# Attention with a checked bound in place of row maxima, three heads at a time on TensorE tiles, and denominators summed on VectorE

## The chip, the core and the metric

The kernel runs on one core of a Trainium2 chip. Times are device microseconds (us) of whole executions. Executions of one kernel spread, so differences of medians of up to some 20 us are read with care. Shorter is better. Engines are named as in the profile: PE is TensorE (matmuls), PEld its weight loads, DVE VectorE, ACT ScalarE, POOL GpSimd, SP SyncE.

## The reference

Two layers over 8 sequences of 1024 tokens with 128 channels, all in fp32. Only the first part of layer 0, attention with four heads of 32 channels, is touched by the change:

```python
def l2norm(t, axis=1, eps=1e-12):                 # axis 1: over the tokens, not the channels
    return t / jnp.clip(jnp.linalg.norm(t, ord=2, axis=axis, keepdims=True), eps)
qkv = jnp.einsum('bxyc,cf->bxyf', x, w_qkv)       # x has been group-normed
q, k, v = ...                                     # (B, 1024, 4 heads, 32)
attn = jnp.einsum('bihd,bjhd->bhij', l2norm(q), l2norm(k)) * 10.0
attn = attn - attn.argmax(axis=-1, keepdims=True) # a shift per row: softmax takes no notice
attn = jax.nn.softmax(attn, axis=-1)
out = jnp.einsum('bhij,bjhd->bhid', attn, v)      # then w_out, b_out and the residual
# [cut: layer 1, a state-space mixer in two directions and a spectral filter]
```

## The kernel before

Attention computes the scores twice: once with queries in rows, only for their row maxima (`peaks`), and once transposed, keys in rows, for the exponentials (`attend`). The negated maxima are written as a 33rd row behind a head's 32 query channels, against a row of ones in the keys, so that the transposed scores come out less their maximum. Behind each head's 32 value channels stand 32 columns of ones, so that the values matmul yields the denominators too.

```python
# peaks: one key-major pass per head for the maxima
sc = ps_s.tile([P, T], F32, tag="s", ...)
for n in range(2):
    nc.tensor.matmul(sc[:, n * 512 : (n + 1) * 512], lhsT=q[rows, h // 2, i * P : (i + 1) * P],
                     rhs=k[rows, h // 2, n * 512 : (n + 1) * 512], start=True, stop=True)
nc.vector.tensor_reduce(top[:, i : i + 1], sc, AX.X, ALU.max, negate=True)
# [cut: the maxima are turned into a row by a diagonal and a one-row matmul]

# attend: two key tiles of one head, half of its queries
rows = slice((h % 2) * 64, (h % 2) * 64 + DH + 1)          # 33 rows
for i in range(2):
    j = 2 * n + i
    nc.tensor.matmul(pt[:, i, :], lhsT=k[rows, h // 2, j * P : (j + 1) * P],
                     rhs=q[rows, h // 2, cols], start=True, stop=True)
nc.scalar.activation(pr, pt, AF.Exp)                        # [shapes cut]
yield
for i in range(2):
    j = 2 * n + i
    nc.tensor.matmul(po, lhsT=v[:, j, h, :], rhs=pr[:, i, :],   # 64 columns: values, ones
                     start=(j == 0), stop=(j == NT - 1))
# [cut: copy, reciprocal of the denominators, product, output projection, residual]
```

Before attention begins, `select_bank` mixes four candidate filter banks for layer 1 on GpSimd, in operations of 128x2048 elements:

```python
def mixed(src, dst, n, tag):
    for i in range(NM):
        part = pool.tile([P, n, C], F32, tag=tag, name=tag)     # one buffer
        nc.sync.dma_start(part, src[i].rearrange("k d e -> d k e"))
        to = dst if i == 0 else part
        nc.gpsimd.tensor_scalar(to, part, w[:, i : i + 1], None, ALU.mult)
        if i:
            nc.gpsimd.tensor_tensor(dst, dst, part, ALU.add)
```

## Time and profile before

| | before |
|---|---|
| time, median of 3 runs | 5078.32 us (5063.51 to 5088.73) |
| span of the profiled execution | 5048.0 us |
| attention, from the start to the fetch of layer 1's filter taps | 2449 us |
| the rest | 2599 us |
| granted PE clock within attention (300 to 550 us) | 0.67 |

The lines of the page that carry this stand in the prediction below.

### The profile page before, as it was taken

The page shows a single profiled execution, that of the slowest core. Times are in us where ns is not written, and L with a number is a line of the kernel's source. Part 1 is how long each engine was busy: PE and PEld are TensorE (multiplying, and loading weights), DVE is VectorE, ACT ScalarE, POOL GpSimd, SP SyncE. Part 2 cuts the span into 40 slices and gives each one's busy share as a digit, 9 for nine tenths or more (in the row PEclk, how much of TensorE's full clock was granted, in tenths as well). Part 3 has the DMA queues.
Part 4 walks back from the last instruction along what each step waited for, and adds up shares of the span by engine and source line. Part 5 has one row for each costly group of instructions (what it writes and reads, how often), then busy time and mean ns, then how long its engine had stood idle before and what let it go on. Part 6 is the DMA issues. An engine that isn't in the chain of part 4 may idle for free.

```text
span 5048.0 us, 32979 instructions
## 1 busy us (share of the span) xinstructions
PE 4862.9 (96%) x12896; PEld 2143.7 (42%) x12896; DVE 1659.0 (33%) x2454; ACT 1102.5 (22%) x1648; POOL 925.7 (18%) x1125
## 2 busy tenths in 40 slices
PE   4999999999999999999889998989999999999999
PEld 1222222222222222222355555555555555555555
DVE  2232322223232222322577777773111111111111
ACT  0111111111111111111456556551010010100100
POOL 7200000000000000000367777671000000000000
PEclk6576676766667666676899999899999999999999
DMA  3000000000000000000100000001000000000000
GB/s 87 13 0 0 4 0 4 0 4 0 0 4 0 0 0 0 0 0 0 34 1 1 1 1 1 1 1 34 5 0 5 1 4 5 1 5 5 1 5 5
DMA packets 31836, 29.37 MB, mean 6 GB/s; under 512 B 4416, under 2 KB 23232, under 8 KB 31680
## 3 DMA queue, kind: packets, MB, share of 16 engines
q1 hardware_dynamic: 31680, 27.26, 1.9%
q8 instruction: 102, 1.67, 0.1%
q14 instruction: 54, 0.44, 0.0%
HBM read 23.06 MB, written 4.19 MB: 5 GB/s over the span
## 4 chain that ended last, share of the span: by engine, by line
PE 87%; POOL 6%; DVE 5%; issue 1%; DMA 1%; ACT 1%; SPq 0%; POOLq 0%; ACTq 0%; DVEq 0%
PE pu L742 22%; PE po L361 15%; PE sc L324 14%; PE pt L349 14%; PE cpo L768 9%; PE sy L647 2%; PE pk L315 2%; PE pl L618 1%; DVE bc L553 1%; DVE xs L553 1%; POOL dau L611 1%; PE sy L649 1%; PE cpo L760 1%; POOL xd L652 1%; PE pp L537 1%
## 5 line engine op out<-in xcount | busy, mean ns | idle before, releaser
L742 PE MATMUL pu<-flt,uk 128*128 128x512 f32 (+3 forms) x4096 | 1183.7, 432 | 0.0
L742 PEld LDWEIGHTS pu<-flt,uk 128*128 128x128 f32 x4096 | 770.4, 189 | 640.6 <-issue 361.8
L361 PE MATMUL po<-pr,v 128*64 128x512 f32 x1024 | 780.2, 896 | 0.0
L324 PE MATMUL sc<-k,q 32*128 32x512 f32 x1024 | 741.7, 858 | 6.4 <-DVE top L331 5.3
L349 PE MATMUL pt<-q,k 33*128 33x512 f32 x1024 | 725.1, 826 | 0.7 <-ACT q L318 0.7
L331 DVE TENSOR_REDUCE top<-sc 128x1 f32<-128x1024 f32 x256 | 310.3, 1212 | 1124.8 <-PE sc L324 1124.4
L753 DVE COPY u<-pu 128x512 f32<-128x512 f32 x256 | 177.0, 691 | 1281.0 <-PE pu L742 1281.0
L357 ACT ACTIVATE pr<-pt 128x1024 f32<-128x1024 f32 x256 | 261.9, 1023 | 1398.6 <-PE pt L349 1398.6
L751 ACT COPY u<-pu 128x512 f32<-128x512 f32 x256 | 149.8, 585 | 1434.4 <-PE pu L742 1434.4
L324 PEld LDWEIGHTS sc<-k,q 32*128 32x128 f32 x1024 | 234.4, 254 | 522.4 <-issue 475.6
L349 PEld LDWEIGHTS pt<-q,k 33*128 33x128 f32 x1024 | 204.8, 231 | 459.9 <-issue 453.0
L361 PEld LDWEIGHTS po<-pr,v 128*64 128x64 f32 x1024 | 157.7, 185 | 554.4 <-issue 537.3
L307 POOL TENSOR_TENSOR diag<-ident,top 128x512 f32<-128x512 f32 x64 | 69.9, 1093 | 1463.2 <-DVE top L331 1463.2
L369 DVE RECIPROCAL den<-av 32x512 f32<-32x512 f32 x64 | 213.8, 3341 | 334.7 <-ACT av L367 334.2
L768 PE MATMUL cpo<-u,m_even 128*128 128x512 f32 x512 | 262.1, 594 | 0.0
L768 PE MATMUL cpo<-u,m_odd 128*128 128x512 f32 x512 | 256.8, 593 | 0.0
L647 PE MATMUL sy<-xdt,lm 128*128 128x64 f32 x1024 | 145.5, 287 | 27.4 <-DVE y L654 27.3
L647 PEld LDWEIGHTS sy<-xdt,lm 128*128 128x128 f32 x1024 | 133.3, 200 | 77.2 <-issue 31.0
L553 DVE SCALAR_TENSOR_TENSOR xs<-xp,cw,xs 128x1024 f32<-128x1024 f32 x96 | 147.0, 1538 | 3.2 <-ACT xs L548 3.2
L608 POOL TENSOR_TENSOR xd<-xb,dsk 128x256 f32<-128x256 f32 x128 | 116.2, 908 | 61.3 <-DVE y L654 42.7
L318 ACT COPY q<-pk 1x512 f32<-1x512 f32 x64 | 36.9, 577 | 371.7 <-PE pk L315 371.7
L716 POOL MEMSET ut<- 128x2 f32 x8 | 0.7, 99 | 604.7 <-PE cpo L760 603.9
(200 smaller groups left out, 4174.3 us busy)
## 6 DMA issues: line engine op xcount, KB each, us to landing
flt<-in_phi_rows SPq DMA_DIRECT2D x4, 1026.0 KB, 10.7
xin<-in_x SPq DMA_DIRECT2D x8, 512.0 KB, 4.0
flt<-in_phi_rows SPq DMA_DIRECT2D x4, 1024.0 KB, 9.5
out<-res SPq DMA_DIRECT2D x8, 512.0 KB, 3.2
part_u<-in_L_ffn_M_u SPq DMA_DIRECT2D x4, 192.0 KB, 2.7
win<-in_L_attn_fwd_in_proj SPq DMA_DIRECT2D x1, 320.0 KB, 6.8
win<-in_L_attn_bwd_in_proj SPq DMA_DIRECT2D x1, 320.0 KB, 3.2
wqkv<-in_L_conv_w_qkv SPq DMA_DIRECT2D x1, 192.0 KB, 2.4
```

Source lines behind the costliest of these rows:

```text
L324: nc.tensor.matmul(sc[:, n * 512 : (n + 1) * 512], lhsT=q[rows, h // 2, i * P : (i + 1) * P], rhs=k[rows, h // 2, n * 512 : (n + 1) * 512] ...
L331: nc.vector.tensor_reduce(top[:, i : i + 1], sc, AX.X, ALU.max, negate=True)
L349: nc.tensor.matmul(pt[:, i, :], lhsT=k[rows, h // 2, j * P : (j + 1) * P], rhs=q[rows, h // 2, cols], start=True, stop=True,)
L357: nc.scalar.activation(pr.rearrange("p i t -> p (i t)"), pt.rearrange("p i t -> p (i t)"), AF.Exp)
L361: nc.tensor.matmul(po, lhsT=v[:, j, h, :], rhs=pr[:, i, :], start=(j == 0), stop=(j == NT - 1))
L369: nc.vector.reciprocal(den, av[DH : 2 * DH, :])
L553: nc.vector.scalar_tensor_tensor(acc, xp[:, at : at + T], cw[d][:, n, i : i + 1], acc, ALU.mult, ALU.add)
L647: nc.tensor.matmul(py[:, 0, hc], lhsT=lm[:, h, :], rhs=xdt[:, hc], start=True, stop=True)
L742: nc.tensor.matmul(pu[:, : HT - j * P], lhsT=uk[:, src, j, :], rhs=rows[:, k % 4, off + j * P : off + HT], start=(j == 0), stop=(j == HB - 1),
L751: nc.scalar.copy(u, pu)
L753: nc.vector.tensor_copy(u, pu)
L768: nc.tensor.matmul(po, lhsT=banks[lag][:, k, :], rhs=u, start=False, stop=last)
```

## The change

Its intent: softmax needs the row maximum only against overflow. The scores are bounded by the norms of the queries and keys, so the exponentials are taken without a shift, the bound is computed beside the rest, and a general copy of the attention and of layer 1 stands behind a branch that is taken if the bound exceeds 20. The queries and keys no longer need a spare row, so four heads fit side by side in 128 rows. Score matmuls of three different heads use three different row groups of PE, values matmuls three different column groups. The ones behind the values are gone; VectorE adds the exponentials up over the key tiles instead, and a matmul with ones sums the rest over the partitions.

```diff
-            for _ in peaks(0, 0, seqs[0]): ...          # [peaks, spare rows, ones behind values: all gone]
+            stream = [(j, h) for j in range(NT) for h in range(HEADS)]
+            groups = [stream[i : i + 3] for i in range(0, len(stream), 3)]
 # scores of one group
+                for i, (j, h) in enumerate(units):
+                    rows = slice(h * DH, (h + 1) * DH)
+                    nc.tensor.matmul(pt[:, i, :], lhsT=k[rows, j * P : (j + 1) * P],
+                                     rhs=q[rows, half * 512 : (half + 1) * 512], start=True, stop=True)
+                nc.scalar.activation(pr, pt, AF.Exp)      # [shapes cut]
 # values of one group, two groups later
+                    nc.tensor.matmul(po[rows, :], lhsT=v[:, j, rows], rhs=pr[:, i, :],
+                                     start=(j == 0), stop=(j == NT - 1))
 # running sums of the exponentials, neighbouring heads of one key tile in one instruction
+                                nc.vector.tensor_tensor(total[:, heads, :], was, pr[:, at : at + run, :], ALU.add)
 # once per half of a sequence
+                    nc.tensor.matmul(pd[h * DH : (h + 1) * DH, :], lhsT=ones[:, :DH], rhs=total[:, h, :], ...)
+                nc.scalar.copy(den, pd)
+                nc.vector.reciprocal(den, den)
+                nc.vector.tensor_tensor(av, av, den, ALU.mult)
 # [cut: the bound per sequence; pieces of the next sequence's preparation go between the groups,
 #  all through one PSUM bank "m"]
+    attention()
+    layer1()
+    with tc.If(nc.values_load(flag[0:1, 0:1]) > 0):
+        attention_general()
+        layer1()
```

## The prediction

> **What bounds the kernel now.** I read the page's busy line and its forty slices first, to see whether one engine carries the span and whether the kernel has stages.
>
> ```profile
> PE 4862.9 (96%) x12896; PEld 2143.7 (42%) x12896; DVE 1659.0 (33%) x2454; ACT 1102.5 (22%) x1648; POOL 925.7 (18%) x1125
> ...
> PE   4999999999999999999889998989999999999999
> ...
> PEclk6576676766667666676899999899999999999999
> ```
>
> TensorE (PE) is busy everywhere; no other engine comes near. The clock row cuts the span in two: in slices 1 to 19 (of 126 us) the granted clock is about 0.66, later 0.9 to 1. The timeline puts the border at 2449 us: there the last attention output is added and the filter taps of layer 1 are fetched. So attention is 2449 us at two thirds clock, layer 1 (2599 us) runs at nearly full clock, and only attention is changed. The change is therefore judged inside those 2449 us.
>
> The groups of instructions say what fills them:
>
> ```profile
> L361 PE MATMUL po<-pr,v 128*64 128x512 f32 x1024 | 780.2, 896 | 0.0
> L324 PE MATMUL sc<-k,q 32*128 32x512 f32 x1024 | 741.7, 858 | 6.4 <-DVE top L331 5.3
> L349 PE MATMUL pt<-q,k 33*128 33x512 f32 x1024 | 725.1, 826 | 0.7 <-ACT q L318 0.7
> L331 DVE TENSOR_REDUCE top<-sc 128x1 f32<-128x1024 f32 x256 | 310.3, 1212 | 1124.8 <-PE sc L324 1124.4
> L357 ACT ACTIVATE pr<-pt 128x1024 f32<-128x1024 f32 x256 | 261.9, 1023 | 1398.6 <-PE pt L349 1398.6
> ```
>
> Three equal blocks: scores for the maxima (sc), scores again transposed (pt), values (po), 2247 us together. Their idle column is zero, that of VectorE (DVE) and ScalarE (ACT) is over 1100 us and released by PE: attention is bound by PE issuing, not by a wait. There are 512 logical matmuls of each kind (8 sequences, 4 heads, 8 key tiles, 2 halves), each two instructions in fp32.
>
> The timeline shows what an instruction costs at each clock:
>
> ```profile
> 1007.69 1.98 PE L324 MATMUL sc<-k,q 32*128 32x512 f32 x4
> ...
> 1009.60 1.98 PE L349 MATMUL pt<-q,k 33*128 33x512 f32 x4
> ...
> 1011.51 1.93 PE L361 MATMUL po<-pr,v 128*64 128x512 f32 x4
> ...
> 1019.62 3.78 PE L324 MATMUL sc<-k,q 32*128 32x512 f32 x4
> ...
> 1023.33 3.67 PE L361 MATMUL po<-pr,v 128*64 128x512 f32 x4
> ```
>
> At full clock four instructions take 1.91 us from start to start of the next block. Single starts lie 0.428 us apart, so 1.71 us is streaming and 0.20 us is lost where the shape changes. At half clock the same four take 3.71 us.
>
> Why half clock with a busy PE? The clock record steps in windows of 3.41 us, and holds only 0.5 and 1. From the trace's matmul records I summed, for each window, streaming time times rows in use (32 or 33 counted by whole groups of 32, over 128). In attention a full-clock window was followed by a full one where this sum was 0.41 or more (135 of 135), and by a half one where its median was 0.35; half-clock windows came back to full at 0.39 to 0.49 and stayed below at a median of 0.27. So here about 0.40 in row use decides; matmuls on 32 rows pull the clock down, the values matmuls on 128 rows (counted fully, though they fill 64 columns) pull it up.
>
> [...]
>
> **The change part by part.** *Removed:* the sc matmuls (741.7 us of PE), their 256 maxima on DVE (310 us, hidden), the diagonals and the one-row matmuls and copies that placed the maxima. *Kept in number:* 512 score and 512 values matmuls, now in groups of three (units run key tile by key tile through heads 0 to 3, so three neighbours always have three different heads: three different row groups for scores, three column groups of 32 for values). The instruction order of the changed kernel confirms it: pt x3, po x3, alternating, with one inserted piece of the next sequence's preparation about every second group.
>
> What does a triple cost? Each logical matmul is two instructions A1, A2 on the same tile[...]. That is four slots instead of two (perfect) or six (none): this is my central choice. A group is then two modes of 4 x 0.428 + 0.20 = 1.91 us, 3.8 us. A half of a sequence has ten triples and one pair (three slots each, 2.97 us): 41 us. Preparation per sequence at full clock: transposes 1.3, q and k 4 x 1.06 = 4.2, values projection 2.1, output projection 2.1, statistics 0.8[...]: 15 us, 7.6 per half. Sum 49 us per half. Weight loads[...] (0.107 us each) might add 0.2 us per mode, 4 us per half; I take half: 51 us.
>
> Clock: row use per group is scores 1.5 slots (0.25, 0.5, 0.5, 0.25) plus values 4 slots, 5.5 x 0.428 / 3.82 = 0.62, above 0.40. So attention should rise from 0.66 to nearly full clock; this is in the numbers above.
>
> Does another engine catch up? DVE per half: 28 sums of 512 columns in 15 instructions, 6 x 0.69 + 5 x 1.22 + 4 x 1.76 = 17.3; a full reciprocal 3.34 (same 512 columns as before, now 16 instead of 64 calls), two 512-column operations 1.4; preparation about 4.9. Sum 27 us. ACT: exponentials 10 x 1.47 (0.58 at 512 and 1.02 at 1024 columns extrapolated) + 1.02, copies 3.5: 19 us. Both lie beside PE's 51.
>
> Start: before, the first transposed scores began at 99.5 us, behind maxima and the filter mixing on GpSimd (POOL). Now nothing but the norms of sequence 0 is needed: about 33 us (they stand early in POOL's new order). But the norms of sequence 1 stand behind the second last filter steps on POOL, which by the old times end near 138 us; so sequence 0 (102 us of PE) ends at 135 and sequence 1 begins at about 143. Then 7 x 2 x 51 = 714, tail with the last output and the flag about 12: 870 us. The bound compared with 20 is 3.9 for the reference's inputs (computed from them), so the general copy is not run[...]. Layer 1 as before 2599. Span 3470; the median time was 30 us over the profiled span (5078 against 5048), so 3500.
>
> **Rivals.** *No overlap of fp32 pairs or of column tiles:* six slots, 2 x (2.57 + 0.20) = 5.5 us a group, 59 + 9 = 68 us per half; sequence 0 ends near 170, then 955: about 3770. For it: nothing in this trace shows overlap.[...] *Full overlap (two slots):* 2.1 us a group, PE 31 us per half; then DVE at 27 with its order among sums, reciprocal and preparation is nearly the bound, and denominators make PE wait for it: some 32 us, 143 + 450 + 12 + 2599 + 30, about 3235.[...] *Clock stays low:* if column tiles count by the columns they fill, use is 3 x 0.428 / 3.82 = 0.34, and the clock would oscillate as now; 51 becomes about 75 and the time 3840. Against: with 64 columns the values matmuls counted in full. *Waits:* single banks for the output and for preparation, and four buffers of exponentials; scores run two groups ahead (7.6 us against 1.5 of exponential), so I expect little.
>
> **Range.** Even the worst of these that I hold likely saves 1200 us, because a third of PE's attention work is gone; slower would need the general branch or a stall that nothing shows. Four slots gets somewhat over half, two slots a quarter, none or low clock a fifth. Predicted 3490 us, range 3230 to 3800; faster 0.98.
>
> **What would show it.** In the changed profile: no sc group; attention ending near 870 us; clock near 1 in its slices; starts of a score triple's six instructions in pairs 0.43 us apart (four slots), not evenly; DVE busy about half of attention; first exponential before 40 us; the layer 1 stage unchanged within 1%. Wrong would be: evenly spaced starts (no overlap), DVE as releaser of PE (full overlap), or half-clock windows among the triples.

Passages that rest on nothing measured here are cut from it, a term of its sum among them. The sum was: a half takes 41 us in groups, and with 7.6 us of preparation 49; 2 us for weight loads make it 51. The cut term is that of the denominators, 4.7 us of the 15 us of preparation per sequence (twice five slots of 0.428 us and 0.20 us). Then 143 + 714 + 12 make about 870 us of attention, with 2599 of the rest 3470, with 30 over the span 3500; 3490 was given. That a triple takes four slots, a pair three and the denominators five was shown by no trace of the kernel before. Its 0.107 us is the distance between the starts of two weight loads there; that they might cost 0.2 us a mode was an estimate, and so was 1.76 us for a sum of 1536 columns, which continues the 0.69 and 1.22 us that 512 and 1024 columns took there.

## More of the kernel before

One view is added here: the busy time of each engine in a stretch well inside attention. The columns are the stretch, its length, then busy time (and instructions) of PE, PEld, DVE, ACT and POOL, the granted PE clock, the DMA share and GB/s.

```profile
300.00:550.00 250.00, 250.00 (x387) 71.25 (x386) 69.38 (x54) 38.18 (x45) 15.44 (x13) 0.67 0.01 2
```

PE had no idle time at all here, and yet its clock was two thirds.

## The result, and the profile after

| | before | after |
|---|---|---|
| time, median of 4 runs each | 5079.84 us (5063.51 to 5088.73) | 3260.35 us (3253.57 to 3272.74) |
| ratio, 95% interval | | 0.643 (0.640 to 0.646) |
| span of the profiled execution | 5048.0 us | 3251.8 us |
| attention ends | 2449 us | 650 us |
| the rest | 2599 us | 2602 us |
| first exponential of scores | 107 us | 36 us |

A ratio is the mean time of one kernel's runs over that of the other's of the same rounds, so it is not quite the ratio of the medians. The result is correct, and the branch was not taken.

The busy line and the slices of the changed kernel (a slice is now 81 us; attention is slices 1 to 8):

```profile
PE 3010.3 (93%) x11876; PEld 1627.5 (50%) x11876; DVE 1400.7 (43%) x2369; ACT 1035.9 (32%) x1488; POOL 832.6 (26%) x1050
...
PE   4489999879989989899899999999999999999999
...
DVE  4377777777777777777631111111111111111111
...
PEclk8789999989999999998899999999999999999999
```

Three things are to be seen. The clock row no longer shows two thirds. PE has holes in slices 1 to 3, digits 4, 4 and 8. DVE is at 7 in the rest of attention, where it was at 2 or 3.

The groups of instructions of attention (busy us and mean ns of one, then the idle time just before them and what ended it):

```profile
L327 ACT ACTIVATE pr<-pt 128x1536 f32<-128x1536 f32 (+1 forms) x176 | 248.6, 1413 | 219.9 <-PE pt L319 207.2
L319 PE MATMUL pt<-q,k 32*128 32x512 f32 x1024 | 236.9, 688 | 51.6 <-DVE q L289 51.6
...
L415 DVE TENSOR_TENSOR total<-total,pr 128x512 f32<-128x512 f32 (+2 forms) x192 | 238.7, 1279 | 24.4 <-ACT pr L327 23.3
L335 PE MATMUL po<-pr,v 128*32 128x512 f32 x1024 | 194.1, 631 | 0.0
```

The sc group is gone. The pt and po groups still have 1024 instructions each, but are busy for 237 and 194 us in place of 725 and 780: a busy time counts overlapping instructions once, so this is overlap (and clock). The score matmuls waited once, for 51.6 us.

The timeline of two groups, first at half clock and then at full clock (start us, length us):

```profile
302.36 2.08 PE L319 MATMUL pt<-q,k 32*128 32x512 f32 x6
...
304.37 1.58 PE L335 MATMUL po<-pr,v 128*32 128x512 f32 x6
...
305.88 1.13 PE L319 MATMUL pt<-q,k 32*128 32x512 f32 x6
...
306.95 1.06 PE L335 MATMUL po<-pr,v 128*32 128x512 f32 x6
```

The single records of the full-clock score triple say how it overlaps. Starts in ns from the span's start:

```
305883  305890  305897        first instruction of each of the three heads
306417  306423  306430        second instruction of each
306947                        first of the values
```

Three start together and, 0.53 us later, three more. (A slot is the time for which one instruction streams, 0.43 us; instructions on different tiles can share one.) Two slots, not four. From start to start a score triple takes 1.06 us, a values triple 0.99 us, in the median of all full-clock groups of the stage.

The same stretch as shown for before:

```profile
300.00:550.00 250.00, 236.42 (x1182) 71.59 (x1182) 187.50 (x199) 136.74 (x123) 15.33 (x26) 0.92 0.02 5
```

PE is now idle for 13.6 of 250 us, the clock is 0.92, and DVE is busy for 75% of the time. A half of a sequence takes 33.9 us here (eleven halves from 218.8 to 592.2 us, by the copies of the outputs); the last sequence, with no preparation of a next one between its groups, takes 25.6 and 22.4.

### The profile page after: what moved, and what is told of

The parts are those of the page before. It is cut to its first block, busy times and chain, and to the rows that moved or that the text cites. A ratio compares the mean times of both kernels' runs of the same rounds, so it can differ in the third digit from the quotient of the medians.

```text
span 3251.8 us, 30443 instructions
## 1 busy us (share of the span) xinstructions
PE 3010.3 (93%) x11876; PEld 1627.5 (50%) x11876; DVE 1400.7 (43%) x2369; ACT 1035.9 (32%) x1488; POOL 832.6 (26%) x1050
## 4 chain that ended last, share of the span: by engine, by line
PE 73%; DVE 11%; POOL 10%; issue 2%; ACT 2%; DMA 1%; SPq 0%; POOLq 0%; DVEq 0%; ACTq 0%
PE pu L976 34%; PE cpo L1002 14%; PE pt L319 4%; PE po L335 3%; PE sy L880 3%; DVE total L415 2%; PE pl L851 2%; DVE xs L786 2%; DVE bc L786 2%; POOL dau L844 2%; DVE den L351 2%; PE sy L882 1%; PE cpo L994 1%; PE pp L770 1%; POOL xd L885 1%
## 5 line engine op out<-in xcount | busy, mean ns | idle before, releaser
L327 ACT ACTIVATE pr<-pt 128x1536 f32<-128x1536 f32 (+1 forms) x176 | 248.6, 1413 | 219.9 <-PE pt L319 207.2
L319 PE MATMUL pt<-q,k 32*128 32x512 f32 x1024 | 236.9, 688 | 51.6 <-DVE q L289 51.6
L415 DVE TENSOR_TENSOR total<-total,pr 128x512 f32<-128x512 f32 (+2 forms) x192 | 238.7, 1279 | 24.4 <-ACT pr L327 23.3
L335 PE MATMUL po<-pr,v 128*32 128x512 f32 x1024 | 194.1, 631 | 0.0
L319 PEld LDWEIGHTS pt<-q,k 32*128 32x128 f32 x1024 | 63.4, 196 | 176.2 <-issue 161.0
L770 PE MATMUL pp<-bxt,win 128*128 128x512 f32 x192 | 103.2, 657 | 2.9 <-ACT xs L781 2.9
L859 DVE TENSOR_TENSOR lm<-lm,gm 128x512 f32<-128x512 f32 x128 | 103.3, 807 | 2.2 <-ACT lm L853 1.2
L869 PE MATMUL pst<-xdd,xb 128*64 128x256 f32 x224 | 76.9, 427 | 29.0 <-POOL xdd L862 22.4
L335 PEld LDWEIGHTS po<-pr,v 128*32 128x32 f32 x1024 | 26.9, 109 | 145.0 <-issue 132.5
L905 PE MATMUL spo<-wo,yts 128*128 128x128 f32 x512 | 93.0, 305 | 5.8 <-DVE gm L858 4.8
```

What stands on the lines that cost most here:

```text
L319: nc.tensor.matmul(pt[:, i, :], lhsT=k[rows, j * P : (j + 1) * P], rhs=q[rows, half * 512 : (half + 1) * 512], start=True, stop=True,)
L327: nc.scalar.activation(pr[:, :n, :].rearrange("p i t -> p (i t)"), pt[:, :n, :].rearrange("p i t -> p (i t)"), AF.Exp)
L335: nc.tensor.matmul(po[rows, :], lhsT=v[:, j, rows], rhs=pr[:, i, :], start=(j == 0), stop=(j == NT - 1))
L415: nc.vector.tensor_tensor(total[:, heads, :], was, pr[:, at : at + run, :], ALU.add)
L770: nc.tensor.matmul(pp[:, i * 512 : (i + 1) * 512], lhsT=win[d][:, DI + n * P : DI + (n + 1) * P], rhs=xt[:, i * 512 : (i + 1) * 512], star ...
```

## The experiments

Eleven kernels were run, all compared with the kernel before on the same chip in the same rounds. "Attention ends" is read at the same place as above, the fetch of layer 1's filter taps; the rest of the span was 2598 to 2622 us in all of them.

| kernel | time, us | ratio to before (95%) | attention ends |
|---|---|---|---|
| after | 3260.35 | 0.643 (0.640 to 0.646) | 650 |
| scores on all 128 rows, work of before | 4285.58 | 0.8465 (0.8416 to 0.8513) | 1683 |
| before without maxima | 3756.36 | 0.7419 (0.7371 to 0.7468) | 1145 |
| after, same head side by side | 3660.79 | 0.7231 (0.7189 to 0.7272) | 1064 |
| after, nearly no sums (wrong) | 3184.34 | 0.6284 (0.6245 to 0.6323) | 580 |
| two heads, denominators on PE | 3533.02 | 0.6957 (0.6903 to 0.7010) | 901 |
| after, two groups a mode | 3254.68 | 0.6409 (0.6379 to 0.6440) | 643 |
| after, filter mixing spread | 3224.61 | 0.6355 (0.6304 to 0.6405) | 623 |
| the same, parts double-buffered | 3227.18 | 0.6346 (0.6313 to 0.6379) | 620 |
| the same, parts on GpSimd's own queue | 3215.22 | 0.6369 (0.6348 to 0.6391) | 606 |
| the same, head 3's later sums on GpSimd | 3206.66 | 0.6331 (0.6317 to 0.6346) | 599 |
| after, head 3's sums on GpSimd | 3253.99 | 0.6427 (0.6411 to 0.6442) | 651 |

### Which part of the gain is the overlap

The order of the units is turned: a head's key tiles one after the other, so that neighbours use the same rows and columns of PE. PE's instructions stay the same in number (11876). VectorE's sums do not: neighbouring units no longer share a key tile, so each is summed alone, in 448 instructions in place of 240. VectorE is busy for only 113 of the 250 us from 300 to 550 us all the same, and PE for all 250, so this is not what sets the time.

```diff
-            stream = [(j, h) for j in range(NT) for h in range(HEADS)]
+            stream = [(j, h) for h in range(HEADS) for j in range(NT)]
```

> The changed kernel with its units ordered head by head, so that the three matmuls of a group share one row group (scores) and one column group (values): same instructions, same groups, same exponentials, no neighbours on different tiles except at the seven places where the head changes. Theory A (the tiles overlap in full, which is what took attention to 649 us): without it a mode takes 6 x 0.428 + 0.20 = 2.77 us instead of about 1.03, a group 5.5 us, a half 59 + 9 = 68 us, attention near 1150 us, time near 3760 us. Rival B (the gain comes from fewer matmuls and the clock, the overlap counts little): within 100 us of 3260. At the head changes the trace also shows how the instructions of two tiles are ordered[...].

Measured: correct, 3660.79 us, attention ends at 1064 us, halves of 61 to 66 us. In the timeline a group in which all three units are of one head:

```profile
497.50 2.84 PE L319 MATMUL pt<-q,k 32*128 32x512 f32 x6
...
500.27 1.90 PE L335 MATMUL po<-pr,v 128*32 128x512 f32 x4
...
502.10 1.98 PE L319 MATMUL pt<-q,k 32*128 32x512 f32 x6
```

Six score instructions now take 2.77 us to the next start (497.50 to 500.27), and a values six 2.69 us. Against 1.06 and 0.99 us that is 2.60 and 2.72 times (by the unrounded medians); three heads side by side save 3.4 us of each such group. The run fixes the slots: six without overlap, two with it.

The step back to the changed kernel is worth 400 us of time, 414 us of attention. The sum of the groups comes to that. In each half 8 triples of one head save 3.4 us; two triples in which the head changes already overlap in part, and with the last pair they save 1.7 us each: 16 x (8 x 3.4 + 3 x 1.7) = 517 us. Of this the changed kernel gives back some 56 us by waits for VectorE (4 us in each of 14 halves, shown below) and 49 us at the start, where the same-head kernel still has work (2.4 us of waiting for sequence 1's queries in place of 51.6). That leaves 412. The expectation, 3760 us, was 100 us too long: it had counted no gain at the changes of head.

The run also settles the prediction's rival that the clock stays low. Its values matmuls fill 32 columns, one after another, and the clock is 0.97 from 300 to 550 us. Counted by rows, use is (6 x 0.428 x 32/128 + 6 x 0.428) / 5.46 = 0.59; counted by the columns filled it would be 0.24, under the limit of 0.40.

The last line is a group with a change of head in it, two units of one head (A, A') and one of the next (B), and it took only 1.91 us. Its single starts:

```
502103 A   502117 B   502637 A   502650 B   503066 A'   503495 A'
```

B is the last of the three in the program, and it started 14 ns after A and 0.95 us before A'. The instructions of different tiles were not started in program order; each tile went through its own. Whether the compiler or the engine reordered them, this trace does not tell. The group's semaphore update stands at B's second instruction (502650), yet the count went up only at 504113, after A' had ended. This order is how six instructions that stand as A A B B C C can fall into two slots.

### Which part is the missing matmuls and the clock

First, the kernel before with the maxima taken out and nothing else: no `peaks`, no spare row, 32 rows in place of 33. (For these inputs the scores are so small that it needs no shift.)

```diff
-            rows = slice((h % 2) * 64, (h % 2) * 64 + DH + 1)
+            rows = slice((h % 2) * 64, (h % 2) * 64 + DH)
-        for _ in peaks(0, 0, seqs[0]):
-            pass
-                if h < HEADS - 1:
-                    top = peaks(b, h + 1, seqs[b])
-                elif b + 1 < B:
-                    top = peaks(b + 1, 0, seqs[b + 1])
```

> The kernel before, with the row maxima alone taken away (no first scores, no maxima, no spare row; heads one after the other, denominators still from ones behind the values on TensorE). Theory A (row use sets the clock): a pair of key tiles is 1.91 us of scores at row use 0.25 and 1.91 us of values at row use 1, mean 0.56, so the clock rises to near 1; 256 x 3.82 = 978 us, preparation about 110, start about 100: attention near 1200, time near 3800 us. Rival B (the clock stays at two thirds with such narrow matmuls): attention near 1700, time near 4350 us.

Measured: correct, 3756.36 us, attention ends at 1145 us, mean clock in it about 0.98. This is 1303 us of the gain (the kernel before was at 5059 us in these rounds), with no tile packing and no VectorE sums. A third of PE's attention work is gone, and the clock rises with it, because what is left is half values matmuls on 128 rows.

Second, the clock alone. All the work of before stays, but the keys get a slot of their own for each head, with zeros in the rows of the other heads, so that both score matmuls contract over all 128 rows:

```diff
-                to = p2.tile([P, 2, T], F32, tag=name, name=f"{name}{b}")
+                slots = 2 if name == "q" else HEADS
+                to = p2.tile([P, slots, T], F32, tag=name, name=f"{name}{b}")
+                nc.gpsimd.memset(to, 0.0)
-                        lhsT=q[rows, h // 2, i * P : (i + 1) * P],
-                        rhs=k[rows, h // 2, n * 512 : (n + 1) * 512],
+                        lhsT=q[:, h // 2, i * P : (i + 1) * P],
+                        rhs=k[:, h, n * 512 : (n + 1) * 512],
```

> The kernel before, all its work kept, but the two kinds of score matmul contract over all 128 rows, with zeros in the keys outside the head's rows: same count of instructions, same columns, same results. Theory A (the granted clock follows the rows in use, at about 0.40): every window of attention is above it, clock near 1; 1316 us of streaming, 154 of shape changes at most, 130 of preparation, 110 of start: attention near 1700 instead of 2449, time near 4330 us. Rival B (the clock follows something else: useful work, columns, power): clock stays near 0.66 and the time within 2% of 5080 us, or gets longer.

Measured: correct, 4285.58 us, attention ends at 1683 us. The clock rows of the two, first without the maxima, then this one:

```profile
PEclk9799999999998999999989899999999999999999
```

```profile
PEclk8899999999999998999999998999999999999999
```

Nothing useful was added, only zeros, and the time fell by 774 us: the clock in attention went from 0.67 to 0.99. (2449 - 107) x 0.67 / 0.99 + 114, with the start at the first exponential of each kernel, gives 1699 for the 1683 seen. So in this kernel the rows in use decide the clock, whatever they hold, as the prediction had read from the records of before.

### Whether VectorE holds PE up

Only the sums of the first two key tiles are left. The result is wrong (relative error 0.13); every other instruction stays.

```diff
-                                nc.vector.tensor_tensor(total[:, heads, :], was, pr[:, at : at + run, :], ALU.add)
+                                if j == 1:
+                                    nc.vector.tensor_tensor(total[:, heads, :], was, pr[:, at : at + run, :], ALU.add)
```

> Wrong result on purpose: the changed kernel without the sums of exponentials on VectorE from the third key tile on (12 of 15 instructions of a half, about 15 of DVE's 27 us; the first sums stay, so that the denominators are still made). Theory A (in the steady part PE sets the pace and DVE lies beside it): a half stays near 34 us, the time falls by at most 30 us, to no less than 3230. Rival B (DVE holds PE up, by the buffers of exponentials, the denominators and the bank that the preparation shares): a half comes to PE's own 29 to 30 us, attention is 55 to 70 us shorter, time near 3195 us.

Measured: 3184.34 us, attention ends at 580 us, 69 us earlier: 36 us because sequence 1's queries were ready at 135.7 us and not at 172.0, the rest in the halves. The stretch of 300 to 550 us:

```profile
300.00:550.00 250.00, 249.56 (x1366) 72.19 (x1360) 92.94 (x119) 160.47 (x142) 12.86 (x29) 1.00 0.01 3
```

PE has no holes, the clock is 1.00, and halves take 29.5 to 30.1 us. So in the changed kernel VectorE holds PE up, by some 4 us of each half. From 300 to 550 us PE's waits in the changed kernel (in total, times, longest) are these two, and without the sums there is none:

```profile
PE pvl L300 <- DVE X L362: 8.2, 4, 2.1
PE pm L246 <- DVE mv L244: 6.3, 4, 3.2
```

That is 14.5 us; a clock of 0.92 in place of 1.00 loses another 20 us of the 250. Over 7.4 halves both make 4.7 us each, an estimate near the 4 us. The chain of waits in the changed kernel shows where (start us, length us):

```profile
422.75 1.46 ACT pr L327
...
424.23 1.90 DVE total L415 x3
426.13 3.26 DVE den L351
...
433.32 1.75 DVE total L415
...
436.60 0.75 DVE q L289
437.36 0.60 DVE X L362
...
438.00 1.57 PE pvl L300 x8
439.57 2.01 PE pt L319 x6
```

At the end of a half VectorE has the last sums, a reciprocal of 3.3 us, more sums and the next sequence's scaling in one queue. The residual sum `X` at its end frees the one PSUM bank that PE's values projection `pvl` waits for. PE itself loses only 2 us there, but in that window of the clock (435.2 to 438.6 us) its row use falls to 0.31, under the limit, and the next groups run at half clock (2.01 us for a triple in place of 1.06). So this short stall cost twice.

### How the clock recovers

The same tiles, but two heads a group, with the ones behind the values as before (64 columns a head) and the denominators on PE: no sums on VectorE at all, but one reciprocal per head. The preparation has two PSUM banks in place of one.

```diff
-            groups = [stream[i : i + 3] for i in range(0, len(stream), 3)]
+            groups = [stream[i : i + 2] for i in range(0, len(stream), 2)]
-                        po[rows, :], lhsT=v[:, j, rows], rhs=pr[:, i, :], start=(j == 0), stop=(j == NT - 1)
+                        po[at : at + 64, h // 2, :], lhsT=v[:, j, h, :], rhs=pr[:, i, :],
+                        start=(j == 0), stop=(j == NT - 1),
```

> The changed kernel without the sums on VectorE: ones behind the values as in the kernel before, so a values matmul fills 64 columns, two heads go side by side instead of three[...], and the reciprocal is taken per head. Right result. Theory A (the sums on VectorE pay because they let three heads lie side by side): 16 groups of 2 x 1.03 to 1.06 us instead of 11, a half 11 us longer, less the denominators' 1.1 us: about 160 us more, time near 3420 us. Rival B (the sums are a cost that PE could have carried): within 40 us of 3260 or faster.

Measured: correct, 3533.02 us, attention ends at 901 us. Halves take 40 us in full-clock stretches and 54 to 59 in others. The stretch of 300 to 700 us:

```profile
300.00:700.00 400.00, 375.99 (x1182) 106.00 (x1180) 168.02 (x138) 150.51 (x161) 17.71 (x29) 0.80 0.01 3
```

This was the most instructive miss. A group takes 1.06 + 1.01 us at full clock and 2.01 + 1.91 at half clock. Row use, counted as in the prediction, is (0.857 x 64/128 + 0.857) / 2.07 = 0.62 at full clock, well above 0.40, and full clock does hold. But the same group at half clock gives 1.285 / 3.92 = 0.33: below the limit, though nothing has changed but the clock. Counted from the records over this run's attention (overlapping instructions on the same rows counted once, a streaming time of 0.428 us a slot at either clock), windows at half clock that stayed at half had a median of 0.32 (101 windows), windows at full clock that stayed at full 0.65 (120). The clock came back 15 times, at 0.36 to 0.51, and 14 of these windows held matmuls of the preparation or the output beside the scores and values. So once a stall has brought the clock down, the stream of two heads a group hardly brings it up again by itself. With three heads the same sum is (0.857 x 96/128 + 0.857) / 3.87 = 0.39 at half clock, just at the limit, and in the changed kernel the clock did come back, at 0.33 to 0.45 (13 windows, median 0.41), and averaged 0.92 from 300 to 550 us. Three heads have no margin, though, and the limit is not a sharp one in these counts.

### Fewer changes of mode

Two score groups and then two values groups, with six buffers of exponentials in place of four, so that the tiling changes half as often.

```diff
-                        catch_up(2)
-                        if g % 2 == 0:
+                        turn += 1
+                        catch_up(2 if turn % 2 == 0 else len(late))
+                        if turn % 2 == 0:
```

> The changed kernel with two score groups and then two values groups in a row, so half as many changes of the tiling mode, and six buffers of exponentials for it. Theory A (a change of mode costs about 0.1 to 0.2 us of PE, 2 x 11 of them in a half, 16 halves): about half of 352 changes fewer, 20 to 35 us less, time near 3230 us. Rival B (the scores then wait for the exponentials, with two score buffers): same or longer than 3260.

Measured: correct, 3254.68 us, attention ends at 643 us. That is the same time as the changed kernel's. Two score triples in a row take 1.92 us and not 2 x 1.06, two values triples 1.84 us and not 2 x 0.99, so PE did save some 0.17 us a group: after two slots of 0.43 us each, 0.21 us of a score triple and 0.13 us of a values triple are left, and in these pairs they are paid once for each change. It spent them waiting for VectorE, 29.4 us from 300 to 550 us in place of 14.5. Its two longest waits there:

```profile
PE pvl L300 <- DVE X L362: 13.4, 4, 3.4
PE pm L246 <- DVE X L362: 12.8, 4, 3.9
```

PE's instructions are not what a half waits for, so fewer changes of mode earn nothing here. The six buffers earned nothing either.

### The start

In the changed kernel, the waits of PE from 30 to 300 us (in total, times, longest):

```profile
PE pt L319 <- DVE q L289: 51.6, 1, 51.6
PE pq L271 <- DVE xc L258: 22.8, 1, 22.8
```

Sequence 1's queries are scaled at 172.0 us. Their factor stands in GpSimd's queue behind the last step of the filter mixing. This kernel cuts the mixing into pieces and queues each piece behind a norm, four pieces per sequence, over the first sequences:

```diff
-            select_bank(p1)
+            bank_work = select_bank(p1)
+            next(bank_work)
+                        if (half, g) in ((0, 0), (0, 7), (1, 5), (1, 8)):
+                            with tc.issue_after(last["pool"].ins):
+                                next(bank_work, None)
```

> The changed kernel, right results, with the mixing of the filter banks on GpSimd cut into pieces that are queued behind the norms of the coming sequence instead of before them. Theory A (sequence 1 waits until 172 us because its norms stand behind that mixing): PE's waits of 52 and 23 us for it go, sequence 1 begins near 100 us, time shorter by 60 to 80 us, near 3190 us. Rival B (the pieces, some 10 us each, delay the norms of every later sequence instead): within 25 us of 3260.

Measured: correct, 3224.61 us (two runs at 3203 to 3204, two at 3245 to 3247), between the two expectations; its interval of ratios just touches the changed kernel's. Attention ends at 623 us and the rest took 2622 us in the profiled run, which is the slowest of the four. Sequence 1's queries come at 83.0 us, 89 us earlier, but only 27 us are left at the end of attention: halves between 145 and 312 us became longer, up to 53 us. The mixing now runs in that stage.

What does it collide with? Two buffers for the parts were tried next, so that a fetch need not wait for GpSimd:

```diff
-                part = pool.tile([P, n, C], F32, tag=tag, name=tag)
+                part = parts.tile([P, n, C], F32, tag=tag, name=tag)   # a pool of two buffers
```

> As the run with the filter mixing in pieces, and two buffers instead of one for the incoming filter parts, so that neither GpSimd nor the loads of the sequences wait for them. Theory A (what that run lost again between 145 and 310 us came from the one buffer): another 20 to 40 us, attention ending near 590 us, time near 3190 us. Rival B (the pieces themselves on GpSimd are in the way): same as that run, near 3225 us.

Measured: correct, 3227.18 us, attention ends at 620 us. No gain that can be told from none. GpSimd waited up to 15.8 us for the next sequence's input (7.5 in the spread kernel), which stands behind the parts in SyncE's queue.

### Sums shared with GpSimd

GpSimd is nearly idle after the mixing. Head 3's running sums are moved there from sequence 1 on, a quarter of VectorE's sums:

```diff
+                                own = run - 1 if b >= 1 and h + run == HEADS else run
+                                if own:
+                                    nc.vector.tensor_tensor(
+                                        total[:, h : h + own, :], was[:, :own, :], pr[:, at : at + own, :], ALU.add)
+                                if own < run:
+                                    nc.gpsimd.tensor_tensor(
+                                        total[:, HEADS - 1, :], was[:, own, :], pr[:, at + own, :], ALU.add)
```

> The changed kernel with head 3's running sums on GpSimd from sequence 1 on (heads 0 to 2 stay on VectorE); nothing else differs. VectorE's sums per half fall from about 17.9 us (7/3 of 1.93+0.69+1.22+1.22+0.69+1.93) to about 13.4. Theory (VectorE's queue holds the preparation up, PE waits for it and the clock falls): halves of sequences 1 to 6 fall by 1 to 3 us, granted clock in 300 to 550 us rises above 0.92, attention ends near 625, time near 3235. Rival (the slowest step of the preparation is a latency that does not depend on the amount of sums, or VectorE and GpSimd slow each other down): halves unchanged or longer, VectorE's mean time of one 1536-column sum above 1.93 us, attention at 650 or later.

Measured: correct, 3253.99 us, attention ends at 651 us; the rival was right. The stretch of 300 to 550 us, and the groups of the two engines in it by shape:

```profile
300.00:550.00 250.00, 229.21 (x1189) 70.06 (x1192) 189.22 (x178) 137.47 (x124) 104.42 (x78) 0.94 0.02 5
```

```profile
L421 POOL TENSOR_TENSOR total<-total,pr 128x512 f32<-128x512 f32 x46 | 79.9, 1736 | 82.4 <-ACT pr L327 81.7
L417 DVE TENSOR_TENSOR total<-total,pr 128x1024 f32<-128x1024 f32 x30 | 44.2, 1472 | 6.5 <-ACT pr L327 6.5
L417 DVE TENSOR_TENSOR total<-total,pr 128x512 f32<-128x512 f32 x30 | 41.6, 1406 | 1.5 <-ACT pr L327 1.5
```

A quarter of the sums left VectorE, and its busy time did not fall (187.50 before, 189.22 now). In the changed kernel a 512-column sum took 0.687 us and a 1024-column one 1.219 us; now they take 1.406 and 1.472. The single records of the stretch hold the control: the 8 running sums of 512 columns that had no GpSimd instruction beside them took 0.68 us, the 22 that had one took 1.67 us in the mean. GpSimd pays as well: over the whole trace its sums took 1.27 us with no VectorE sum beside them (26) and 1.88 us with one (72). The detail of the expectation, that the 1536-column sum would grow, was wrong: it took 1.81 us (1.89 in the changed kernel). What makes the two slow each other down, no run here shows.

It bears on the slow halves of the spread mixing too. From 100 to 320 us of the next section's second kernel, where the mixing runs beside the sums, the 13 running sums of 512 columns with no GpSimd instruction beside them took 0.68 us, the 8 with one 2.12 us. All sums there took 133 us; at their unhindered times they would take 96. These 37 us are an estimate, near the 33 us that six halves of this stage lost against 33.9 us each. That the sums are the cause is not shown.

### Put together

Two more kernels combine what was learnt. In both, the parts are fetched through GpSimd's own queue; the first also has head 3's sums on GpSimd from sequence 4 on, after the mixing, the second does not.

```diff
-                nc.sync.dma_start(part, src[i].rearrange("k d e -> d k e"))
+                nc.gpsimd.dma_start(part, src[i].rearrange("k d e -> d k e"))
```

> Everything that helped put together: the filter mixing in pieces spread over the first sequences with double-buffered parts, the parts now fetched from GpSimd's own queue so that they do not stand before the next sequence's input on SyncE's queue, and head 3's sums on GpSimd from sequence 4 on. Theory: sequence 1's queries near 83 us as in the spread kernel, no slow halves at 145 to 312 us from late inputs, later halves 1 to 3 us shorter than in the changed kernel; attention ends near 590, time near 3190. Rival (GpSimd's pieces and the preparation's norms still wait for each other, whatever the queue): halves at 145 to 312 us stay above 40 us, attention at 615 to 625, time at 3220 as before.

> The kernel with everything put together, but with all running sums back on VectorE: so it differs from the spread kernel with double-buffered parts only in the queue that fetches the parts, GpSimd's own. Theory (the queue made the gain, head 3's sums on GpSimd gave nothing, as when they were moved alone): time within 0.3% of 3207 or a little below, later halves as in the changed kernel (33 to 36 us), attention end 590 to 605. Rival (the sums on GpSimd made the gain): time near 3227 and attention end near 620, with waits of GpSimd for the next input of 15 us still there.

Measured: 3206.66 us (3204.49 to 3212.41) with the sums, 3215.22 us (3207.39 to 3230.98) without. Both are correct. Attention ends at 599 and 606 us. GpSimd's longest wait for an input, 15.8 us in the double-buffered kernel, is 7.4 and 12.9 us. The first lands between its two expectations: the halves between 145 and 312 us stay long (up to 47.6 us), as the rival said, but attention ends earlier than it allowed, and the 3190 of the theory was not reached. The longest wait of PE in that stage is now one of 11.4 us for the statistics in VectorE's queue.

The second is within the 0.3% that its theory gave (0.27%), but it does not decide. Its attention ends just outside the 590 to 605 of the theory, its wait of 12.9 us is near the rival's 15, and its executions overlap those of the double-buffered kernel (3214.59 to 3243.20 us). They were run at other times. Against the kernel before, its ratio is even the higher of the two, 0.6369 against 0.6346, with overlapping intervals. The profiled run was its fastest, that of the double-buffered kernel its slowest, so the ends of attention, 606 and 620 us, do not decide it either. So it is not shown that the queue earned anything, nor that the sums on GpSimd earned the other 8 us.

What is shown is the first kernel as a whole. It has the lowest median of the correct kernels: 54 us or 1.6% below the changed one (the intervals of their ratios lie apart), and 47 us below the kernel with head 3's sums on GpSimd, which ran in the same rounds on the same chip.

## Why the prediction was right or wrong

The time of 3260.35 us lies in the range of 3230 to 3800, near its low end, 230 us below the predicted 3490. That it lies there is owed to the range, which took in the rival of full overlap: the case that the prediction held likeliest did not come true. Two of the signs that it had named for being wrong appeared, VectorE as releaser of PE and half-clock windows among the triples. By its steps:

**What bounds before, and what is removed: right.** Taking the maxima alone out gave 1303 us. The row-use reading of the clock was right too, and is now shown by a run: zeros in the unused rows took the clock from 0.67 to 0.99. PE was busy for 250 of 250 us at the 0.67; streaming alone is 4 x 0.428 / 1.91 = 0.90 of a block.

**"That is four slots instead of two (perfect) or six (none): this is my central choice": wrong.** The triple takes two slots. The trace of the same-head kernel shows the third unit's instruction starting before the second's, on a tile of its own. A mode costs 1.06 or 0.99 us, not 1.91; a group 2.05, not 3.8.

**"51 us per half": wrong by that step.** It is 33.9. Eleven groups at 2.05 us or a little less, and 7.6 us of preparation as predicted, make 30 us of PE; that is what the kernel without sums takes (29.5 to 30.1). The other 4 us are VectorE's.

**"Both lie beside PE's 51": true of 51, wrong of 30.** The sum of VectorE's work was right: 27 us predicted, 187.50 / 250 x 33.9 = 25.4 measured. ScalarE's was too: 19 predicted, 18.5 measured. With PE at 30, 25 us of VectorE in a fixed order are enough to make PE wait at the end of each half, and the clock falls at most of these waits (7 of the 8 from 300 to 550 us). The rival "Full overlap" had this, with 32 us per half.

**The start: too early by 29 us.** "Sequence 1 begins at about 143" rested on the norms standing behind no more than the second last filter steps. In the trace GpSimd computes the inverse norms at 155.1 us, then four more filter steps of 16.0 us together, then the product of the norms at 171.8 us. The term was mis-sized, the mechanism (GpSimd's queue) was the right one.

**"The median time was 30 us over the profiled span": wrong reading.** The profiled execution of after took 3253.57 us for a span of 3251.8, so a run is 1.8 us longer than its span. The 30 us were the distance between one execution and the median of others. Here the median is 8.6 us above the span.

**Clock, flag, layer 1, first exponential: right in the main.** Clock mostly at 1 (0.92 in the steady part), with half-clock windows after stalls that were not predicted; branch not taken; 2602 against 2599 us; 36 us against "before 40".

The sum: attention was put at 870 and ended at 650. Of these 220 us, the start takes back 29, and 14 halves after it save 14 x (51 - 33.4) = 246 (33.4 is their mean, the last two included); the tail was 10 us and not 12. The wrong addition gives another 21; layer 1 takes back 3, and 3490 was already 10 below the sum. "Full overlap" was given a quarter of the chances, at 3235. It was 25 us too low: the start was 29 too early and the 14 halves 18 too short, against an addition 21 too large.

Where the 1820 us came from, by the runs: 1303 from dropping the maxima, clock included; 96 from the step to the same-head kernel; 400 from there to the changed kernel, by overlap. These add up to 1799, because the kernel before was at 5059 us in the rounds of the two experiments. The 96 were not taken apart: grouping, denominators and start all change there, and the triples in which the head changes overlap already, so a part of the overlap's gain is in them.

What stays open: why exactly the spread mixing leaves the halves from 145 to 312 us long. Slower sums beside GpSimd could account for it by the estimate above, but no run had the mixing without the sums in that stage. Open too are whether the queue of the parts matters, and whether the compiler or the engine set the order in which matmuls on different tiles start.

## What to carry to other kernels

Narrow matmuls on different row or column groups of PE overlapped completely here even where each is two instructions (a score triple took 1.06 us in place of 2.77, a values triple 0.99 in place of 2.69), so cost them by tile and not in program order, and then add up the other engines again: one that was far below the bound can become it (VectorE was busy for 69 of 250 us before and for 188 after). The clock followed the row use here and was easier to keep than to regain (the stream of two heads a group counts 0.62 at full clock and 0.33 at half, with a limit near 0.40), so count a stream's row use at half clock as well, and treat a short stall of PE as a long one (after a wait of 2 us the next triples took 2.01 us in place of 1.06). Before moving work between VectorE and GpSimd, ask what will run beside it on the other: a 512-column sum on VectorE took 0.68 us alone and 1.67 us beside a GpSimd instruction, one on GpSimd 1.27 us alone and 1.88 us beside a VectorE sum.
